# A causal convolution by 128-column blocks: a second level of three products for four, its shared product drained by ScalarE and GpSimd

## The chip, the cores and the metric

The kernel runs on one core of a Trainium2 chip. The metric is device time in microseconds (us), the median of several runs. TensorE (PE in the profile) multiplies, VectorE (DVE) and ScalarE (ACT) do elementwise work, GpSimd (POOL) does small work and issues some DMAs, SyncE (SP) issues the others. One execution was also recorded by the hardware profiler; all durations of single instructions come from that one.

## The reference, cut to what matters

The input x has 2048 rows of 1024. After a layer norm, two branches are added to x: a feed-forward layer with int4 weights, and a causal convolution along each row with one kernel K of 1024 taps, which is computed from small state-space parameters.

```python
K = _s4_kernel(Lambda, p, q, B, Ct, step, L).astype(u.dtype)
n = 2 * L
y = jnp.fft.irfft(jnp.fft.rfft(u, n=n) * jnp.fft.rfft(K, n=n), n=n)[..., :L]
return y + D[0] * u
...
x = x + _L0_attn_ref(xn, ...) + _L0_ffn_ref(xn, ...)
```

Written as a matrix product, output column block j (128 columns) of a row is the sum over k up to j of input block k times a 128x128 block that depends on j - k alone.

## The kernel before, in words

Every large product is made of float16 pairs: a float32 value is kept as a high half and a low half, and a product takes three matmuls (high by high, high by low, low by high; the list PASS). The kernel has three stages. The first computes the norm, the gate and the up projection and the hidden layer, the second the convolution, the third the down projection. The second stage is the one that changes: `conv` and `last_tiles` (lines 1215 and 1240) in the loop of lines 1275 to 1297.

The convolution works on 32 output tiles of 128 rows by 512 columns. They are numbered by cp (which 1024 rows), c (which 512 of these), hh (which half of the columns) and q (which 128 rows). The transposed normalised input `xc` holds, for each 512 rows and each half, four blocks of 128 columns. `band` (line 1185) holds the convolution's taps laid out so that a run of its columns is a row of neighbouring blocks of the matrix.

A tile is built in two steps. `conv` takes a PSUM bank (`cv`) and adds the part of the output that comes from the same half: input block k goes to all the columns from 128k on, so the matmuls are 512, 384, 256 and 128 columns wide, three of each. For the upper half (hh = 1) it also adds what comes from the lower half. That is a product of two by two blocks of 256, done with three products: two with differences of the taps (`diff`, lines 1205 to 1209), twelve matmuls of 256 columns, in the same bank, and one with the sums of the inputs, `xs`, in a bank of its own (`cc`, lines 1254 to 1258, six matmuls of 256 columns). `last_tiles` adds the last 64 and 128 rows of the down projection to the bank `cv` (five matmuls of 512 columns, `hpl` by `wp`), loads the tile of x into `o` (named p in the profile), and VectorE adds the bank to it (line 1252). For the upper half VectorE then adds the bank `cc` to both 256-column halves of `o` (line 1260). SP stores `o`.

Two loops order this. In the first 1024 rows (cp = 0) `last_tiles` of a tile stands four tiles behind its `conv`; in the second it follows at once, and after each group of four tiles `prepare` brings up operands of the third stage. The sums `xs` for all of cp stand before the loop, four calls of `add_split` (line 1193: three additions, a copy on ScalarE, a subtraction).

The order in which each engine's instructions stand is decided before the run by a planner: in this part of the program nothing is pinned, and the planner goes through its own expected times and puts next what it expects to be ready, with the order of the program as the priority.

The buffers that matter: eight PSUM banks under one tag (line 1123); ten buffers `hb` for 512 float32 columns (line 1122), from which the two `diff`, all temporaries `t` and all tiles `o` are taken; six `f` buffers for `x7`, `xs` and the factors `a` and `s` of the third stage (line 1118); five `g` buffers, one of which holds `hpl` in the second 1024 rows (line 1119); three `be` buffers, which hold `band` and the two `wp` (line 1120).

The third stage is a list of 49 products of 60 matmuls of 256 columns each. Product (1, 6), the third of them, needs the sum of two factors (line 1166), which takes a fifth `f` buffer after the four factors.

Of the kernel before, what the change touches and what calls it, by code (L numbers as in the profile page):

```python
# [24 lines left out]
F16 = mybir.dt.float16  # L25
# [3 lines left out]
AF = mybir.ActivationFunctionType  # L29
# [58 lines left out]
def build(nc, tc, x, xp, raw_d, sz_d, par_d, vct_d, tab_d, csrow_d, out):  # L88
# [3 lines left out]
    with es:  # L92
# [15 lines left out]
        def htile(name, tag="h"):  # L108
            return pools["h"].tile([P, 512], F32, tag=tag, name=name)
# [1074 lines left out]

        band = bep.tile([P, 2, 1024], F16, tag="be", name="band")
        for b in range(2):
# [6 lines left out]
        def add_split(dst, srcs, op):  # L1193

            (h0, l0), (h1, l1) = srcs
            n = dst.shape[2]
            t = htile("t")[:, 0:n]
            V.tensor_tensor(t, h0, h1, op)
            V.tensor_tensor(t, t, l0, ALU.add)
            V.tensor_tensor(t, t, l1, op)  # L1200
            A.copy(dst[:, 0], t)
            V.tensor_tensor(dst[:, 1], t, dst[:, 0], ALU.subtract)


        diff = []
        for a0, b0 in ((128, 384), (640, 384)):
            a, b = ([band[:, i, c : c + 384] for i in range(2)] for c in (a0, b0))
            diff.append(htile(f"diff{a0}").bitcast(F16).rearrange("p (a b) -> p a b", a=2)[:, :, 0:384])
            add_split(diff[-1], (a, b), ALU.subtract)
        wp = []  # L1210
        for i in range(2):
            wp.append(bep.tile([P, 2, 1024], F16, tag="be", name=f"wp{i}"))
            SP.dma_start_transpose(wp[i].rearrange("p b (c d) -> p (b c) d", d=P), WPN[:, i])

        def conv(cp, c, hh, q, xc):

            ts = slice(q * P, (q + 1) * P)
            ps = bank(f"cv{cp}{c}{hh}{q}")
            first = [True]

            def mm(dst, w, m):
                PE.matmul(dst, w, m, start=first[0], stop=False, skip_group_check=True)
                first[0] = False

            xt = xc[2 * c + hh]
            for k in range(4):
                for xi, bi in PASS:
                    mm(ps[:, P * k : 512], xt[:, xi, k, ts], band[:, bi, 0 : 512 - P * k])
            if hh:

                xt = xc[2 * c]
                for k in range(2):
                    for xi, bi in PASS:
                        mm(ps[:, 0:256], xt[:, xi, k + 2, ts], diff[0][:, bi, P - P * k : P - P * k + 256])
                for k in range(2):
                    for xi, bi in PASS:
                        mm(ps[:, 256:512], xt[:, xi, k, ts], diff[1][:, bi, P - P * k : P - P * k + 256])
            return ps

        def last_tiles(ps, cp, c, hh, q, hpl, xs):  # L1240

            ts = slice(q * P, (q + 1) * P)
            cols = slice(512 * hh, 512 * hh + 512)
            mm = lambda w, m, stop=False: PE.matmul(ps, w, m, start=False, stop=stop, skip_group_check=True)
            for hi, wi in PASS:
                mm(hpl[:, c, hi, ts], wp[0][:, wi, cols])
            mm(hpl[:, c, 2, ts], wp[1][:, 0, cols])
            mm(hpl[:, c, 2, ts], wp[1][:, 1, cols], True)
            t0 = 1024 * cp + 512 * c + P * q
            o = htile(f"p{cp}{c}{hh}{q}")  # L1250
            SP.dma_start(o, x[t0 : t0 + P, cols])
            V.scalar_tensor_tensor(o, ps, osc, o, ALU.mult, ALU.add)
            if hh:
                pc = bank(f"cc{cp}{c}{q}")
                for k in range(2):
                    for n, (xi, bi) in enumerate(PASS):
                        PE.matmul(pc[:, 0:256], xs[:, c, xi, k, ts], band[:, bi, 512 - P * k : 768 - P * k],
                                  start=(k == 0 and n == 0), stop=(k == 1 and n == 2))
                ov = o.rearrange("p (a b) -> p a b", a=2)
                V.scalar_tensor_tensor(  # L1260
                    ov, pc[:, 0:256].unsqueeze(1).to_broadcast([P, 2, 256]), osc, ov, ALU.mult, ALU.add)
            SP.dma_start(out[t0 : t0 + P, cols], o)
# [12 lines left out]
        for cp in range(2):  # L1275
# [5 lines left out]
            xc = [xf[cp, 3], xf[cp, 1], x7, xf[cp, 0]]  # L1281
            xs = fp.tile([P, 2, 2, 2, 512], F16, tag="f", name=f"xs{cp}")
            for c in range(2):
                for k in range(2):
                    a, b = ([xc[2 * c][:, i, m, :] for i in range(2)] for m in (k, k + 2))
                    add_split(xs[:, c, :, k, :], (a, b), ALU.add)

            behind = []
            for c, hh in ((0, 0), (0, 1), (1, 1), (1, 0)) if cp == 0 else ((0, 1), (0, 0), (1, 1), (1, 0)):
                for q in range(4):  # L1290
                    behind.append((conv(cp, c, hh, q, xc), cp, c, hh, q))
                    if len(behind) > 4 - 4 * cp:
                        last_tiles(*behind.pop(0), hpl, xs)
                if cp:
                    prepare()
            while behind:
                last_tiles(*behind.pop(0), hpl, xs)

# [206 lines left out]
```

## Time and profile before

| what | us |
|---|---|
| median of 3 runs | 1290.91 (1290.76 to 1292.72) |
| the profiled execution, its own time | 1293.54 |
| its span, first to last instruction | 1291.5 |
| PE busy in the span | 1258.9 (97%) |
| DVE busy | 1007.7 (78%) |
| ACT busy | 672.1 (52%) |
| POOL busy | 177.4 (14%) |
| first and last start of a matmul into `cv` | 846.6 and 966.1 |

The span is shorter than the execution's time by 2.0 us, which lie around it. "Busy" counts the time in which at least one instruction of the engine was under way. Matmuls overlap in the record: one of 512 columns is shown with 379 ns, though the next starts 216 ns later, so it is the distance of starts that tells what a matmul costs in a row of matmuls. The convolution stage lies between about 846 and 967 us of the span. There GpSimd does nothing, and ScalarE is busy for a tenth of the time.

### The profile page before, as it was taken

What the parts mean: (1) busy time and instruction counts of PE and PEld (TensorE: products, weight loads), DVE (VectorE), ACT (ScalarE), POOL (GpSimd) and SP (SyncE); (2) the same over time, 40 slices, a digit from 0 to 9 for tenths busy, and PEclk for the clock granted to TensorE, in tenths of its full rate; (3) what the DMA queues carried; (4) which work ended last, traced back from release to release, by engine and by line L of the source; (5) the groups of instructions that cost most, each with busy time, mean ns of one, the idle gap of its engine ahead of it and who ended that gap; (6) DMA issues with size and microseconds to landing.
All of it is one profiled execution on the core that took longest, in us unless ns stands there. A gap on an engine that the chain in (4) does not pass through costs nothing. (4 is left out here: it accounts for less than half of the span.)

```text
span 1291.5 us, 20871 instructions
## 1 busy us (share of the span) xinstructions
PE 1258.9 (97%) x7880; PEld 753.2 (58%) x7880; DVE 1007.7 (78%) x1344; ACT 672.1 (52%) x1208; POOL 177.4 (14%) x267
## 2 busy tenths in 40 slices
PE   5999999999999999999998999999999999999998
PEld 5744344444444444444443444456668888888887
DVE  6789974888978788878788887663758898779792
ACT  4868476666657556656666675620105433443330
POOL 2230010200010000100010001000000131356440
PEclk8999999999999999999999999999999999999999
DMA  6692938789795959889998998775938778999981
GB/s 222 147 227 59 203 101 157 213 218 239 162 252 144 253 146 241 224 209 235 244 239 216 260 243 201 226 264 183 350 122 344 239 230 226 256 283 259 288 176 50
DMA packets 358401, 276.04 MB, mean 214 GB/s; under 512 B 211668, under 2 KB 304668, under 8 KB 354204
## 3 DMA queue, kind: packets, MB, share of 16 engines
q1 hardware_dynamic: 335676, 261.59, 74.1%
q0 software_dynamic: 21760, 10.49, 6.9%
q10 hardware_dynamic: 864, 2.62, 0.5%
q8 instruction: 62, 1.02, 0.3%
q14 instruction: 39, 0.32, 0.1%
HBM read 132.36 MB, written 94.84 MB: 176 GB/s over the span
## 5 line engine op out<-in xcount | busy, mean ns | idle before, releaser
L82 PEld LDWEIGHTS <-wf 128*128 128x128 f16 x2807 | 274.0, 98 | 341.0 <-issue 7.0
L77 PEld LDWEIGHTS <-g 128*128 128x128 f16 x2940 | 287.7, 98 | 33.5
L82 ACT ACTIVATE w<-w,sz 128x64 f32<-128x64 int32 x560 | 196.0, 428 | 68.4 <-DVE w L82 51.3
L77 ACT CAST g<-a 128x2560 f16<-128x2560 f32 x42 | 97.5, 2324 | 176.6 <-PE A L77 50.4
L82 PE MATMUL D<-x,wf 128*128 128x512 f16 x816 | 188.0, 380 | 0.9 <-ACT D L82 0.9
L77 PE MATMUL A<-b,g 128*128 128x256 f16 x1680 | 185.9, 273 | 0.0
L82 PE MATMUL A<-x,wf 128*128 128x512 f16 x791 | 177.7, 380 | 5.1 <-DMA wf<-nat 4.7
L82 PE MATMUL C<-x,wf 128*128 128x512 f16 x804 | 179.1, 379 | 0.0
L82 DVE TENSOR_TENSOR w<-w 128x256 f32<-128x256 f32 (+1 forms) x244 | 132.6, 544 | 39.5 <-ACT w L82 32.3
L77 PEld LDWEIGHTS <-wf 128*128 128x128 f16 x1152 | 100.1, 100 | 98.4 <-DMA wf<-nat 4.3
L77 DVE TENSOR_TENSOR g<-a,g 128x2560 f16<-128x2560 f32 x42 | 118.5, 2823 | 29.6 <-ACT g L77 29.6
L1357 POOL DMA_DIRECT2D out<-o x64 | 78.8, 2127 | 320.7 <-DVE o L77 309.8
L82 ACT CAST nd<-w 128x896 f16<-128x896 f32 x70 | 65.2, 932 | 82.8 <-DVE w L82 65.6
L322 POOL TENSOR_SCALAR sz<-sz 128x16 f32<-128x16 f32 x42 | 16.5, 392 | 632.8 <-DMA sz<-in_sz 586.5
L77 PE MATMUL D<-b,g 128*128 128x256 f16 x840 | 94.0, 273 | 0.0
L82 PE MATMUL B<-x,wf 128*128 128x512 f16 x396 | 90.9, 379 | 2.1 <-ACT B L82 2.1
L82 DVE TENSOR_TENSOR nd<-w,nd 128x896 f16<-128x896 f32 x70 | 76.1, 1086 | 9.2 <-ACT nd L82 9.2
L82 ACT CAST nat<-w 128x896 f16<-128x896 f32 x62 | 55.2, 936 | 34.1 <-ACT B L82 17.0
L77 PEld LDWEIGHTS <-x 128*128 128x128 f16 x576 | 53.4, 98 | 25.0 <-issue 1.1
L82 DVE TENSOR_TENSOR nat<-w,nat 128x896 f16<-128x896 f32 x62 | 64.8, 1085 | 1.5 <-ACT nat L82 1.5
L77 PE MATMUL cv<-band,x 128*128 128x512 f16 (+3 forms) x384 | 57.1, 299 | 1.0 <-DVE hb L82 1.0
L77 DVE SCALAR_TENSOR_TENSOR p<-cv,p 128x512 f32<-128x512 f32 x32 | 22.0, 689 | 43.3 <-PE cv L77 33.6
(169 smaller groups left out, 1408.6 us busy)
## 6 DMA issues: line engine op xcount, KB each, us to landing
a<-HF SPq DMA_DIRECT2D x28, 1280.0 KB, 8.0
WD<-nd SPq DMA_DIRECT2D x70, 448.0 KB, 4.1
b<-WD SPq DMA_DIRECT2D x49, 640.0 KB, 6.0
w<-SZT SPq DMA_DIRECT2D x80, 256.0 KB, 5.4
raw<-in_raw SPq DMA_DIRECT2D x65, 256.0 KB, 4.0
HF<-ha SPq DMA_DIRECT2D x54, 256.0 KB, 3.4
HF<-s SPq DMA_DIRECT2D x40, 256.0 KB, 2.8
HF<-hb SPq DMA_DIRECT2D x36, 256.0 KB, 3.6
```

The lines of the kernel that those rows point to most:

```text
L77: return method(*args, **kw)
L82: self.last = method(*args, **kw)
L322: G.tensor_scalar(sz[:, 0], sz[:, 0], WS, None, ALU.mult)
L1357: G.dma_start(dst, o[:, q], accum_op=ALU.add)
```

## The change

The two by two block products of 256 columns are split once more, into 128-column blocks with three products in place of four.

In `conv`, the own half is now computed directly only inside each 256-column block (matmuls of 256, 128, 256 and 128 columns, three of each). What goes from the first 256 columns to the second is a two by two block product, made of two products with the difference tables `near` (in `last_tiles`, six matmuls of 128 columns by `crossed`) and one shared product with the sum of two input blocks. For the upper half, each of the two products with `diff` is split in the same way: twelve matmuls of 128 columns with `far[0]` and `far[1]` in `conv`, and two shared products. All shared products, six matmuls of 256 and nine of 128 columns for an upper tile and three of 128 for a lower one, go to a second bank (`cc`), now for each tile.

That bank is no longer read by VectorE. ScalarE copies it, scaled, into a new buffer `u` from the `hb` pool, and GpSimd adds `u` to `o` (two additions over 512 columns for an upper tile, one over 256 for a lower one), before VectorE adds the bank `cv`.

The tables `near` and `far` are made by `outer_less_middle` (three subtractions and additions of 256 columns, a copy on ScalarE, a subtraction), in the spare columns of the `be` buffers. The sums of inputs are made by `block_sums`: five per 512 rows of cp and c, in one `f` buffer for each c; the one for c = 0 stands before the loop, the one for c = 1 before the second group of tiles. A sum is one addition of the high halves, a copy on ScalarE, a subtraction, and two additions in float16.

```diff
--- before.py
+++ after.py
@@ -1182,7 +1182,12 @@
             return gsplit(src, f"g{k}_{m}"), b
 
 
-        band = bep.tile([P, 2, 1024], F16, tag="be", name="band")
+        def table(name):
+
+            t = bep.tile([P, 2560], F16, tag="be", name=name)
+            return t[:, 0:2048].rearrange("p (a b) -> p a b", a=2), t[:, 2048:2560].rearrange("p (a b) -> p a b", a=2)
+
+        band, near = table("band")
         for b in range(2):
             for n in range(2):
                 p0 = 64 * b + 32 * n
@@ -1193,72 +1198,112 @@
         def add_split(dst, srcs, op):
 
             (h0, l0), (h1, l1) = srcs
-            n = dst.shape[2]
-            t = htile("t")[:, 0:n]
+            t = htile("t")[:, 0:384]
             V.tensor_tensor(t, h0, h1, op)
             V.tensor_tensor(t, t, l0, ALU.add)
             V.tensor_tensor(t, t, l1, op)
             A.copy(dst[:, 0], t)
             V.tensor_tensor(dst[:, 1], t, dst[:, 0], ALU.subtract)
 
-
+        def outer_less_middle(dst, src):
+
+            t, sub = htile("t")[:, 0:256], ALU.subtract
+            t3 = t.rearrange("p (a b) -> p a b", a=2)
+            part = [src[:, i].rearrange("p (k d) -> p k d", d=P) for i in range(2)]
+            mid = [part[i][:, 1:2].to_broadcast([P, 2, P]) for i in range(2)]
+            V.tensor_tensor(t3, part[0][:, 0:3:2], mid[0], sub)
+            V.tensor_tensor(t3, t3, part[1][:, 0:3:2], ALU.add)
+            V.tensor_tensor(t3, t3, mid[1], sub)
+            A.copy(dst[:, 0], t)
+            V.tensor_tensor(dst[:, 1], t, dst[:, 0], sub)
+
+        wp, far = [], []
         diff = []
         for a0, b0 in ((128, 384), (640, 384)):
             a, b = ([band[:, i, c : c + 384] for i in range(2)] for c in (a0, b0))
             diff.append(htile(f"diff{a0}").bitcast(F16).rearrange("p (a b) -> p a b", a=2)[:, :, 0:384])
             add_split(diff[-1], (a, b), ALU.subtract)
-        wp = []
+        outer_less_middle(near, band[:, :, 128:512])
         for i in range(2):
-            wp.append(bep.tile([P, 2, 1024], F16, tag="be", name=f"wp{i}"))
-            SP.dma_start_transpose(wp[i].rearrange("p b (c d) -> p (b c) d", d=P), WPN[:, i])
+            w, f = table(f"wp{i}")
+            wp.append(w)
+            far.append(f)
+            SP.dma_start_transpose(w.rearrange("p b (c d) -> p (b c) d", d=P), WPN[:, i])
+            outer_less_middle(f, diff[i])
+
+        def block_sums(cp, c, xc):
+
+            sm5 = fp.tile([P, 5, 2, 512], F16, tag="f", name=f"xs{cp}{c}")
+            lower, upper = xc[2 * c], xc[2 * c + 1]
+            add = ALU.add
+            for i, (xt, a, b) in enumerate(((lower, 0, 1), (upper, 0, 1), (lower, 2, 3), (lower, 0, 2), (lower, 1, 3))):
+                dst, t = sm5[:, i], htile("t")
+                t16 = t.bitcast(F16)[:, 0:512]
+                V.tensor_tensor(t, xt[:, 0, a], xt[:, 0, b], add)
+                A.copy(dst[:, 0], t)
+                V.tensor_tensor(dst[:, 1], t, dst[:, 0], ALU.subtract)
+                V.tensor_tensor(t16, xt[:, 1, a], xt[:, 1, b], add)
+                V.tensor_tensor(dst[:, 1], dst[:, 1], t16, add)
+            return sm5
+
+        def crossed(ps, xt, k, col, pair, ts):
+
+            for xi, bi in PASS:
+                for n in range(2):
+                    c0 = col + P * n
+                    PE.matmul(ps[:, c0 : c0 + P], xt[:, xi, k + 1 - n, ts], pair[:, bi, P * n : P * n + P],
+                              start=False, stop=False, skip_group_check=True)
 
         def conv(cp, c, hh, q, xc):
 
             ts = slice(q * P, (q + 1) * P)
             ps = bank(f"cv{cp}{c}{hh}{q}")
-            first = [True]
-
-            def mm(dst, w, m):
-                PE.matmul(dst, w, m, start=first[0], stop=False, skip_group_check=True)
-                first[0] = False
-
             xt = xc[2 * c + hh]
             for k in range(4):
-                for xi, bi in PASS:
-                    mm(ps[:, P * k : 512], xt[:, xi, k, ts], band[:, bi, 0 : 512 - P * k])
+                lo, hi = P * k, 256 * (k // 2) + 256
+                for n, (xi, bi) in enumerate(PASS):
+                    PE.matmul(ps[:, lo:hi], xt[:, xi, k, ts], band[:, bi, 0 : hi - lo],
+                              start=(k == 0 and n == 0), stop=False, skip_group_check=True)
             if hh:
-
-                xt = xc[2 * c]
-                for k in range(2):
-                    for xi, bi in PASS:
-                        mm(ps[:, 0:256], xt[:, xi, k + 2, ts], diff[0][:, bi, P - P * k : P - P * k + 256])
-                for k in range(2):
-                    for xi, bi in PASS:
-                        mm(ps[:, 256:512], xt[:, xi, k, ts], diff[1][:, bi, P - P * k : P - P * k + 256])
+                crossed(ps, xc[2 * c], 2, 0, far[0], ts)
+                crossed(ps, xc[2 * c], 0, 256, far[1], ts)
             return ps
 
-        def last_tiles(ps, cp, c, hh, q, hpl, xs):
+        def last_tiles(ps, cp, c, hh, q, hpl, xc, xs):
 
             ts = slice(q * P, (q + 1) * P)
             cols = slice(512 * hh, 512 * hh + 512)
             mm = lambda w, m, stop=False: PE.matmul(ps, w, m, start=False, stop=stop, skip_group_check=True)
+            pc = bank(f"cc{cp}{c}{hh}{q}")
+            shared = [(256, 0, band[:, :, 256:384])]
+            if hh:
+                shared = [(384, 1, band[:, :, 256:384]), (256, 2, diff[0][:, :, P : 2 * P]), (384, 0, diff[1][:, :, P : 2 * P])]
+                for k in range(2):
+                    for n, (xi, bi) in enumerate(PASS):
+                        PE.matmul(pc[:, 0:256], xs[:, 3 + k, xi, ts], band[:, bi, 512 - P * k : 768 - P * k],
+                                  start=(k == 0 and n == 0), stop=False, skip_group_check=True)
+            for i, (col, src, w) in enumerate(shared):
+                for n, (xi, bi) in enumerate(PASS):
+                    PE.matmul(pc[:, col : col + P], xs[:, src, xi, ts], w[:, bi],
+                              start=(not hh and n == 0), stop=(i == len(shared) - 1 and n == 2), skip_group_check=True)
+            crossed(ps, xc[2 * c + hh], 0, 256, near, ts)
             for hi, wi in PASS:
                 mm(hpl[:, c, hi, ts], wp[0][:, wi, cols])
             mm(hpl[:, c, 2, ts], wp[1][:, 0, cols])
             mm(hpl[:, c, 2, ts], wp[1][:, 1, cols], True)
             t0 = 1024 * cp + 512 * c + P * q
-            o = htile(f"p{cp}{c}{hh}{q}")
+            o, u = htile(f"p{cp}{c}{hh}{q}"), htile(f"u{cp}{c}{hh}{q}")
             SP.dma_start(o, x[t0 : t0 + P, cols])
+            used = slice(0, 512) if hh else slice(256, 384)
+            A.activation(u[:, used], pc[:, used], AF.Copy, scale=osc)
+            ov = o.rearrange("p (a b d) -> p a b d", a=2, b=2)
+            if hh:
+                G.tensor_tensor(o.rearrange("p (a b) -> p a b", a=2), o.rearrange("p (a b) -> p a b", a=2),
+                                u[:, 0:256].unsqueeze(1).to_broadcast([P, 2, 256]), ALU.add)
+                G.tensor_tensor(ov, ov, u[:, 256:512].rearrange("p (a d) -> p a d", a=2).unsqueeze(2).to_broadcast([P, 2, 2, P]), ALU.add)
+            else:
+                G.tensor_tensor(ov[:, 1], ov[:, 1], u[:, 256:384].unsqueeze(1).to_broadcast([P, 2, P]), ALU.add)
             V.scalar_tensor_tensor(o, ps, osc, o, ALU.mult, ALU.add)
-            if hh:
-                pc = bank(f"cc{cp}{c}{q}")
-                for k in range(2):
-                    for n, (xi, bi) in enumerate(PASS):
-                        PE.matmul(pc[:, 0:256], xs[:, c, xi, k, ts], band[:, bi, 512 - P * k : 768 - P * k],
-                                  start=(k == 0 and n == 0), stop=(k == 1 and n == 2))
-                ov = o.rearrange("p (a b) -> p a b", a=2)
-                V.scalar_tensor_tensor(
-                    ov, pc[:, 0:256].unsqueeze(1).to_broadcast([P, 2, 256]), osc, ov, ALU.mult, ALU.add)
             SP.dma_start(out[t0 : t0 + P, cols], o)
 
         items = [(k, m) for k in SEQ for m in (1, 2, 6, 5, 7, 4, 3)]
@@ -1279,22 +1324,22 @@
             x7 = fp.tile([P, 2, 4, 512], F16, tag="f", name=f"x7_{cp}")
             SP.dma_start(x7, XSP[cp])
             xc = [xf[cp, 3], xf[cp, 1], x7, xf[cp, 0]]
-            xs = fp.tile([P, 2, 2, 2, 512], F16, tag="f", name=f"xs{cp}")
-            for c in range(2):
-                for k in range(2):
-                    a, b = ([xc[2 * c][:, i, m, :] for i in range(2)] for m in (k, k + 2))
-                    add_split(xs[:, c, :, k, :], (a, b), ALU.add)
-
+            xs = {0: block_sums(cp, 0, xc)}
             behind = []
-            for c, hh in ((0, 0), (0, 1), (1, 1), (1, 0)) if cp == 0 else ((0, 1), (0, 0), (1, 1), (1, 0)):
+            order = ((0, 0), (0, 1), (1, 1), (1, 0)) if cp == 0 else ((0, 1), (0, 0), (1, 1), (1, 0))
+            for i, (c, hh) in enumerate(order):
+                if i == 1:
+                    xs[1] = block_sums(cp, 1, xc)
                 for q in range(4):
                     behind.append((conv(cp, c, hh, q, xc), cp, c, hh, q))
                     if len(behind) > 4 - 4 * cp:
-                        last_tiles(*behind.pop(0), hpl, xs)
+                        b = behind.pop(0)
+                        last_tiles(*b, hpl, xc, xs[b[2]])
                 if cp:
                     prepare()
             while behind:
-                last_tiles(*behind.pop(0), hpl, xs)
+                b = behind.pop(0)
+                last_tiles(*b, hpl, xc, xs[b[2]])
 
 
         U = [uxp.tile([P, 4, 512], F32, tag="ux", name=f"U{cp}") for cp in range(2)]
```

## The prediction

> **What bounds the kernel now.** I read the page first, for the engines' shares:
>
> ```profile
> PE 1258.9 (97%) x7880; PEld 753.2 (58%) x7880; DVE 1007.7 (78%) x1344; ACT 672.1 (52%) x1208; POOL 177.4 (14%) x267
> ```
>
> TensorE is busy for 97% of the span, but that is an average over stages, so next the table of windows over the convolution (window, length, then busy time and instructions of PE, PEld, DVE, ACT and POOL, then clock, DMA share, GB/s):
>
> ```profile
> 846.00:857.00 11.00, 9.83 (x71) 6.10 (x69) 8.30 (x16) 2.84 (x5) 0.00 (x0) 1.00 0.79 269
> 857.00:860.00 3.00, 2.89 (x19) 1.70 (x20) 3.00 (x7) 0.00 (x0) 0.00 (x0) 1.00 0.94 294
> ...
> sum 121.00, PE 119.72 PEld 78.15 DVE 71.02 ACT 12.73 POOL 0.00; mean PE 9.21 PEld 6.01 DVE 5.46 ACT 0.98 POOL 0.00
> ```
>
> TensorE idles for 1.28 us of 121, all of it before 857.2, at full clock. The stage costs what its matmuls cost. Their prices are distances of starts in the timeline of TensorE (start, length, what, count):
>
> ```profile
> 896.23 1.79 PE L77 MATMUL cv<-band,x 128*128 128x512 f16 x12
> 897.86 1.24 PE L77 MATMUL cv<-wp,hpl 128*128 128x512 f16 x5
> 898.94 0.82 PE L77 MATMUL cc<-band,xs 128*128 128x256 f16 x6
> 899.60 1.79 PE L77 MATMUL cv<-band,x 128*128 128x512 f16 x12
> ```
>
> Five of 512 columns take 897.86 to 898.94: 0.216 us each. Six of 256 take 0.66: 0.109 each. For 128 columns there is a run of 48 early in the kernel:
>
> ```profile
> 50.49 0.83 PE L77 MATMUL g<-x,wf 128*128 128x128 f16 x12
> 51.16 0.83 PE L77 MATMUL u<-x,wf 128*128 128x128 f16 x12
> 51.83 0.83 PE L77 MATMUL g<-x,wf 128*128 128x128 f16 x12
> 52.50 0.83 PE L77 MATMUL u<-x,wf 128*128 128x128 f16 x12
> ```
>
> Twelve take 0.67: 0.056 each. The twelve matmuls of an own half take 1.63, which leaves 0.162 for 384 columns. So a matmul costs its columns and some 0.003 us, although each has a weight load of its own.
>
> **TensorE's sum.** A lower tile before: 3 x (0.216 + 0.162 + 0.109 + 0.056) + 5 x 0.216 = 2.71 us. An upper tile has 18 of 256 columns more: 4.67. Sixteen of each: 118.1. A lower tile after: own half 6 x 0.109 + 6 x 0.056 = 0.99; shared product and `near` 9 x 0.056 = 0.50; `wp` 1.08; together 2.57. An upper one: 0.99; crossed 12 x 0.056 = 0.67; bank `cc` 6 x 0.109 + 9 x 0.056 = 1.16; `near` 0.34; `wp` 1.08; together 4.24. Sixteen of each: 109.0. That is 384 more matmuls, and **-9.2 us** if nothing else comes late.
>
> A page of the Trainium skill speaks against the change here: TensorE: Matmul & The Clock Gate, section Back-to-back issue gap, says that a stream of pairs of weight load and matmul at 128 columns sustains about 81 ns each. By it the 672 added matmuls of 128 columns would cost 16.8 us more, and the change would lose 7.6 us on TensorE alone. The run above has a weight load per matmul and shows 56 ns; the measurement decides.
>
> **VectorE and ScalarE in the middle of the stage: hidden.** VectorE's operations on 512 float32 columns start 0.60 apart when nothing holds them (903.14, 903.74, 904.34 in its timeline). Gone are 16 additions of bank `cc` (9.6 us) and 32 operations for `xs` (19.2). Added are 20 sums: two operations of 0.60 each, and two all in float16, a form that the trace has at 1024 columns (0.69 against 1.22 for float32), so about 0.35: 1.9 in all, 38 us. The three tables add 12 operations of 256 columns at 0.34: 4.1. So +13 us on 71 of 118. ScalarE gets 32 copies `u` (0.43 to 0.60, its rows of 64 and 512 columns) and 15 more casts (0.51 to 0.62): +24 us on 13. TensorE's work covers both, except at the start.
>
> **GpSimd: hidden, if an addition stays well under 2.8 us (rival 3).** It has no row of this size. The nearest:
>
> ```profile
> L323 POOL TENSOR_TENSOR sz<-sz 128x16 f32<-128x16 f32 x42 | 15.7, 376 | 3.2
> L125 POOL TENSOR_SCALAR_AFFINE_SELECT ident<-ident 128x128 f32<-128x128 f32 x1 | 0.3, 282 | 0.1
> ```
>
> From below: VectorE's 0.60 for 512 columns. Taken: four times the 128-column row, 1.13. From above: twice that for the second input, 2.26, and 0.9 us of waiting, since the 128x16 addition takes 0.22 alone and up to 1.12 under VectorE: 3.2. At 1.13 an upper tile needs 2.26 of GpSimd's time against 4.24 of TensorE's, a lower one 0.6 against 2.57. VectorE's last addition queues behind GpSimd's on the way to the store, and SP's queue, which issues stores and loads in order, behind that; eight banks at two a tile leave some three tiles of slack.
>
> **The start: where part of the gain is lost.** From the timeline of all engines:
>
> ```profile
> 847.18 10.70 SPq L77 DMA_DIRECT2D p<-in_x  x4
> 849.40 6.68 PE L77 MATMUL cv<-band,x 128*128 128x512 f16 x48 [1.01 <-DVE hb L82]
> 850.64 0.55 DVE L77 TENSOR_TENSOR t<-band 128x384 f32<-128x384 f16 x1
> 857.11 1.25 PE L77 MATMUL cv<-wp,hpl 128*128 128x512 f16 x5 [0.27 <-DMA hpl<-HPL]
> 861.04 0.69 DVE L77 SCALAR_TENSOR_TENSOR p<-cv,p 128x512 f32<-128x512 f32 x1
> ```
>
> The load of `hpl` ends at 857.1 whatever the convolution does, and until then TensorE lives on own halves: five of 1.63, and seven matmuls with `diff`. After the change an own half is 0.99. In program order tiles 0 to 5 with two banks `cc` fill the eight banks, so six own halves, 5.9 us, last from 846.6 (with the 1.0 of idle that is there) to 853.6. `far` and `near` are not ready: VectorE starts on the tables at 850.64 and needs 3.8 us for `diff` and 4.1 for the rest. So TensorE idles 3.5 us in place of 0.27: **+3.3** (0.3 less if all eight banks take own halves, which ends at 855.5: +1.4 is the lower end).
>
> Then the banks. All ten sums of cp = 0 stand ahead of the first last addition in the program: VectorE has them done at 850.64 + 3.8 + 4.1 + 19 = 877.5. The temporaries also stand ahead of the first `o` and `u` in the ten buffers. That this order binds is shown by the second 1024 rows: all 16 loads of p stand ahead of the next temporary, which waited for a store:
>
> ```profile
> 898.49 0.69 DVE L77 TENSOR_TENSOR t<-x 128x512 f32<-128x512 f16 x1 [2.02 <-DMA out<-p]
> ```
>
> So `o` of tile 0 is loaded when the third sum is done, at about 864, lands at 868 (3.7 us is the loads' median), and its bank comes free between 869 and 878. TensorE has, with the bank that `u` of tile 0 frees at 866, work until about 870.5; a second `cc` gives it three more. It loses between 0 and 4.6 us. Before, the first last addition (861.04) came among the sums and 2.8 us after its matmuls, so neither end is plain; I take the middle, **+2.3**.
>
> **The handover.** Before, the sum `s` for product (1, 6) starts at 955.7, when `xs` is dead. After, `xs` and x7 live to the last tile, so it starts about 1.4 us before the stage ends. Three operations of 2.73, one last addition of 0.6, a cast of 2.3 and a subtraction of 2.8 end 12.5 us after the stage; the product is due after two others, 2 x 6.55 = 13.1. I take **+0.3**; bounds 0 and 2.
>
> **Sum.** -9.2 + 3.3 + 2.3 + 0.3 = -3.3 us. The profiled execution took 1293.54 (span 1291.5 and 2.0 around it), so it would become 1290.2. It lies 2.6 above the median of the runs; the same step from 1290.91 gives **1287.6**.
>
> **Rivals.**
> 1. The start stays covered: own halves fill eight banks (+1.4), last additions slip in among the sums (0), the handover costs nothing: -7.8, 1283.1. For it: the planner puts next what is ready. Against: VectorE's list at the start more than doubles. Chance 0.22.
> 2. The start eats it all: VectorE runs its sums to the end, 3.3 + 4.6, and the handover takes 1.3: 0.0, 1290.9. For it: program order is the priority, and the sums are always ready. Chance 0.17.
> 3. Slower: GpSimd becomes the bound of the upper tiles. At p us for an addition of 512 columns an upper tile needs 2p and a lower one p/2, 40p in all, against TensorE's 109. Single upper tiles outlast TensorE's 4.24 from 2.1 on, which the lower ones and the slack of three tiles make good; the whole is slower than before once 40p exceeds 109 + 3.3, from 2.8. At 2.9 that is 116 - 109 - 3.3 = +3.7, 1294.6; at the upper bound of 3.2, +15.7, 1306.6. For it: the 128x16 addition goes from 0.22 to a mean of 0.38 beside VectorE. Against: it needs 2.5 times my price. Chance 0.20, most of it near the lower end.
> That the change does not do what it says is hardly a case: the columns are counted from the code.
>
> **Numbers.** The forecast's own range is -1 to -5.5, chance 0.41. A measurement of this kernel can tell about 0.2%, 2.6 us, from no change. Faster than that: rival 1 and three quarters of the forecast, 0.52; within it: the rest of the forecast, rival 2 and a little of rival 3, 0.29; slower: 0.19. The range reaches from rival 1 to the milder half of rival 3: 1282.5 to 1296.
>
> **What would show it.** Right: starts of 128-column matmuls 0.056 apart in the stage, the starts of the last tile's matmuls 3 to 4 us earlier than 966.1 in the span, idle of TensorE before 857.1 near 4 to 5 us and some more before 880, GpSimd additions near 1.1 us, VectorE not waiting for GpSimd with a full queue behind. Wrong: 128-column matmuls at more than 0.07; idle of TensorE spread over the stage, with GpSimd above 9 tenths (rival 3); no idle after 857 (rival 1); a hole ahead of product (1, 6) of over 2 us.

## The result, and the profile after

The changed kernel takes **1309.7 us** (median of 4 runs, 1306.71 to 1309.91) where the kernel before took 1291.26 beside it (4 runs): ratio **1.0136, 95% interval 1.0118 to 1.0153**. The forecast was 1287.6 with a range up to 1296. The profiled execution took 1309.75 with a span of 1307.8: 16.3 more than the span before.

Lines of the page of the changed kernel: the engines' shares, and the granted clock by fortieths of the span.

```profile
PE 1259.5 (96%) x8264; PEld 767.2 (59%) x8264; DVE 1024.4 (78%) x1388; ACT 694.2 (53%) x1255; POOL 239.9 (18%) x315
...
PEclk8999999999999999999999999979999999999999
```

TensorE is busy as long as before, with 9 us less to do. The dip of the clock row lies in the convolution. The table of windows over that stage, columns as in the prediction:

```profile
846.00:857.00 11.00, 4.62 (x52) 4.10 (x52) 8.73 (x18) 3.40 (x6) 0.00 (x0) 0.88 0.97 339
857.00:860.00 3.00, 2.96 (x22) 2.40 (x21) 3.00 (x7) 2.19 (x5) 0.00 (x0) 0.50 0.04 10
860.00:870.00 10.00, 8.24 (x50) 4.66 (x50) 10.00 (x24) 2.69 (x6) 0.00 (x0) 0.60 0.08 26
...
940.00:950.00 10.00, 5.62 (x47) 4.11 (x46) 9.31 (x13) 4.74 (x5) 6.15 (x4) 0.82 1.00 344
```

Before, TensorE was busy for 9.83 of the first eleven microseconds at full clock; now for 4.62, and from 854.3 to 868.0 it runs at half clock. A second gap lies at 940 to 950.

**The account used below.** From each matmul of the stage to the next I take the distance of starts less the price of its columns (0.216, 0.162, 0.109, 0.056 us for 512, 384, 256 and 128). What is left is lost time, and I add it up over four parts: start (the first 30 us of the stage), middle (30 to 58), late (58 to the end), third (the first 25 us of the third stage). It holds idle time and slow clock together. Before: 1.6, 0, 0, 0. Changed: **13.6, 5.1, 8.3, 2.2**. So 27.6 us more are lost, TensorE's own sum is 9.2 less, and the stage began 1.9 earlier (844.7; it begins between 841 and 850 in the profiles here, from what lies ahead of it): 16.5, against 16.3 in the span.

The start in TensorE's timeline:

```profile
847.43 4.12 PE L77 MATMUL cv<-band,x 128*128 128x256 f16 x48 [1.62 <-DVE hb L82]
856.50 0.39 PE L77 MATMUL cc<-band,xs 128*128 128x128 f16 x2 [4.95 <-ACT xs L77]
...
860.63 0.58 PE L77 MATMUL cv<-wp,x 128*128 128x128 f16 x4 [0.68 <-ACT wp L77]
862.34 0.58 PE L77 MATMUL cv<-band,x 128*128 128x128 f16 x4 [1.12 <-DVE band L77]
862.72 2.34 PE L77 MATMUL cv<-wp,hpl 128*128 128x512 f16 x5
864.85 0.63 PE L77 MATMUL cv<-band,x 128*128 128x128 f16 x4
```

Five own halves are done at 851.6. Then TensorE waits 4.95 us for the first sum, and for shorter times for the tables (`far` is in `wp`, `near` in `band`). The four holes are 8.4 us (1.3 in the kernel before). Behind 862.34 TensorE waits for nothing until 883.0. The other 5.2 are slow matmuls: the five of 512 columns at 862.72 take 2.13 to the next start, 0.426 each, twice their price. The granted clock was half from 854.3 to 868.0.

GpSimd's rows over the stage (busy, mean ns of one, then idle before and its releasers), and what VectorE's last additions waited for (total, times, longest):

```profile
L1303 POOL TENSOR_TENSOR p<-p,u 128x512 f32<-128x512 f32 x16 | 21.5, 1350 | 0.6
L1301 POOL TENSOR_TENSOR p<-p,u 128x512 f32<-128x512 f32 x16 | 20.6, 1296 | 27.3 <-ACT u L77 22.1 <-DMA p<-in_x 5.2
L1305 POOL TENSOR_TENSOR p<-p,u 128x256 f32<-128x256 f32 x16 | 20.1, 1254 | 88.2 <-DMA p<-in_x 75.7 <-ACT u L77 6.1 <-issue 3.7
```

```profile
DVE p L77 <- POOL p L1303: 37.3, 12, 7.1
...
DVE p L77 <- POOL p L1305: 11.6, 9, 2.7
...
PE cv L77 <- DVE p L77: 6.4, 2, 4.4
```

GpSimd works 62 us of 136, so it is not the bound, but VectorE's last additions wait 49 us for it, and TensorE twice for them. The longer of those two, in the timeline of all engines:

```profile
942.21 4.23 DVE L77 TENSOR_TENSOR t<-x 128x512 f32<-128x512 f16 x3
...
942.77 3.38 POOL L1303 TENSOR_TENSOR p<-p,u 128x512 f32<-128x512 f32 x2
...
946.96 0.68 DVE L77 SCALAR_TENSOR_TENSOR p<-cv,p 128x512 f32<-128x512 f32 x1
...
947.69 2.72 PE L77 MATMUL cv<-band,x 128*128 128x256 f16 x18 [4.38 <-DVE p L77]
```

The operations of VectorE's sums (`t`) and GpSimd's additions run at once and slow each other. The row of three `t` holds two of float32, which took 1.16 and 1.75 us in place of 0.69, and one of float16, 1.48 in place of 0.41; GpSimd's additions took 1.7 each in place of 1.26 (one at 936.97 with no sum beside it). The last addition that frees the bank comes behind the sums, at 946.96. Undisturbed, the three `t` start 0.60, 0.60 and 0.34 apart, 1.5 us in place of the 4.15 to the next start, so some 2.6 of the 4.38 us are their own delay (an estimate).

### The profile page after: what moved, and what is told of

The parts are those of the page before. It is cut to its first block, busy times and chain, and to the rows that moved or that the text cites. A ratio compares the mean times of both kernels' runs of the same rounds, so it can differ in the third digit from the quotient of the medians.

```text
span 1307.8 us, 21862 instructions
## 1 busy us (share of the span) xinstructions
PE 1259.5 (96%) x8264; PEld 767.2 (59%) x8264; DVE 1024.4 (78%) x1388; ACT 694.2 (53%) x1255; POOL 239.9 (18%) x315
## 5 line engine op out<-in xcount | busy, mean ns | idle before, releaser
L77 PEld LDWEIGHTS <-x 128*128 128x128 f16 x768 | 58.0, 102 | 20.1 <-issue 12.2
L77 PE MATMUL cv<-band,x 128*128 128x128 f16 (+1 forms) x576 | 56.2, 247 | 9.3 <-DVE p L77 6.4
```

The source lines that it names most:

```text
L77: return method(*args, **kw)
```

## The experiments

All medians stand beside runs of the kernel before on the same chip (medians 1291.3 to 1293.4), so ratios are compared. The account is of the one profiled execution of each kernel, which can lie off the median: e13's took 1295.50 (its stage began at 850.1, the latest of all), e10's 1302.94, e2's 1305.91, e7's 1294.03. `*` marks kernels with the old start.

| kernel | median us | ratio (95%) | start, middle, late, third |
|---|---|---|---|
| changed | 1309.70 | 1.0136 (1.0118-1.0153) | 13.6, 5.1, 8.3, 2.2 |
| e1_vector_drain | 1299.83 | 1.0040 (1.0025-1.0055) | 13.4, 0, 6.3, 0.3 |
| e2_13_buffers | 1308.41 | 1.0107 (1.0087-1.0127) | 15.3, 1.3, 6.5, 3.2 |
| e3_late_sums | 1304.30 | 1.0080 (1.0060-1.0100) | 11.4, 1.4, 9.2, 0.8 |
| e4_first_tiles_old * | 1298.24 | 1.0033 (1.0020-1.0046) | 1.7, 4.3, 7.6, 0.8 |
| e5_old_start_vector * | 1293.63 | 0.9993 (0.9983-1.0002) | 1.7, 6.1, 1.3, 0.3 |
| e6_old_start_vector_13 * | 1288.61 | 0.9960 (0.9944-0.9977) | 1.2, 1.7, 1.1, 0.3 |
| e7_no_gpsimd_add | 1296.42 | 1.0021 (1.0011-1.0031) | 12.3, 0, -0.1, 0.1 |
| e8_old_start_13 * | 1292.54 | 0.9993 (0.9981-1.0005) | 1.2, 0, 4.0, 4.8 |
| e9_before_13 | 1292.36 | 0.9997 (0.9986-1.0007) | 1.5, 0, 0, 0 |
| e10_gpsimd_aside | 1298.56 | 1.0042 (1.0025-1.0059) | 13.5, 4.0, 2.3, 0.1 |
| e11_first_four_old | 1299.04 | 1.0041 (1.0028-1.0054) | 9.8, 4.1, 2.4, 0.3 |
| e12_bank_first | 1308.10 | 1.0119 (1.0104-1.0134) | 12.5, 4.6, 8.8, 0.5 |
| e13_bank_first_old_start_13 * | 1289.49 | 0.9972 (0.9962-0.9982) | 1.1, 0, 5.4, 0.8 |
| e14_bank_first_13 | 1301.75 | 1.0068 (1.0051-1.0086) | 16.7, 0, 6.0, 1.1 |
| e15_bank_first_old_start * | 1297.21 | 1.0036 (1.0023-1.0050) | 1.6, 3.0, 7.6, 1.0 |
| e16_own_u * | 1296.16 | 1.0033 (1.0023-1.0044) | 2.0, 1.9, 8.6, 0.8 |
| e17_four_by_vector * | 1290.51 | 0.9989 (0.9977-1.0000) | 1.2, 0, 5.8, 0.9 |

**The start: e3, e4, e11.**

e3_late_sums makes the sums of the second 512 rows one group of tiles later:

```diff
-                if i == 1:
+                if i == 2:
                     xs[1] = block_sums(cp, 1, xc)
```

e4_first_tiles_old computes the first eight tiles (cp = 0, c = 0) as the kernel before did: with wide matmuls and `diff`, without `near`, `far` and the first three sums; a lower tile needs no bank `cc`:

```diff
+            if cp == 0 and c == 0:
+                for k in range(4):
+                    for n, (xi, bi) in enumerate(PASS):
+                        PE.matmul(ps[:, P * k : 512], xt[:, xi, k, ts], band[:, bi, 0 : 512 - P * k],
...
+                            PE.matmul(ps[:, 256 * part : 256 * part + 256], xc[2 * c][:, xi, k + 2 - 2 * part, ts],
...
```

e11_first_four_old is e6 (below) with only the first four, lower, tiles the old way, and all five sums at the start.

> Only the second set of five sums is moved one group of tiles later in the program, behind the first four last additions. If the sums' place ahead of the last additions holds up the first loads and banks: the 5 us between 875 and 902 go, in the second 1024 rows the sums may come too late by as much: 1303 to 1307. If the start is lost to the tables and the first five sums alone: 1308 to 1311.

> The first eight tiles (first 512 rows) are computed as before the change: own halves directly, two products with the differences over 256 columns, no near or far, two sums in place of five; the rest as after the change. This gives TensorE its old cover at the start and costs 2.3 us of the matmuls' gain. Theory A (the start costs 12 us, half clock included): no hole over 1.5 us before 875, no half clock there, 1298 to 1302. Rival (the loss is made in the middle by GpSimd and buffers): 1308 to 1312.

> As the fastest so far (VectorE drains, thirteen buffers), but only the first four tiles, all lower ones, are computed as before the change, in place of eight; all five sums stand at the start again. 1.7 us less of TensorE's work. If the start needs cover for the own halves alone: 1285 to 1288. If tables and five sums must have come before the upper tiles' part of it: 1290 to 1296, with a hole before 870.

e4 takes the loss of the start from 13.6 to 1.7 us. TensorE's timeline there is that of before again, with full clock throughout:

```profile
854.39 0.93 PE L77 MATMUL cv<-diff,x 128*128 128x256 f16 x7
855.65 0.82 PE L77 MATMUL cv<-wp,hpl 128*128 128x512 f16 x3 [0.34 <-DMA hpl<-HPL]
```

e3, which only takes five sums out of the way, brings 2.2 back at the start. It also takes the middle loss from 5.1 to 1.4, with ten buffers and with GpSimd's additions as they were: the place of the sums in VectorE's list is part of that loss too. In e11 the own halves last, but the upper tiles' table (`far`) is still late, and the time, 1299.04, is above both of the ranges that were expected:

```profile
868.36 2.62 PE L77 MATMUL cv<-wp,x 128*128 128x128 f16 x24 [4.42 <-DVE wp L77]
```

So the start needs long matmuls for as long as VectorE makes tables and sums, not only until `hpl` lands.

**Who adds the shared products: e1, e7, e10.**

e1_vector_drain has no `u` and nothing on GpSimd; VectorE reads the bank in three additions (one for a lower tile):

```diff
+                V.scalar_tensor_tensor(o2, pc[:, 0:256].unsqueeze(1).to_broadcast([P, 2, 256]), osc, o2, ALU.mult, ALU.add)
+                for i in range(2):
+                    w = pc[:, 256 + P * i : 384 + P * i].unsqueeze(1).to_broadcast([P, 2, P])
+                    V.scalar_tensor_tensor(ov[:, i], w, osc, ov[:, i], ALU.mult, ALU.add)
...
```

e7_no_gpsimd_add leaves GpSimd's three additions away, and e10_gpsimd_aside makes additions of the same size inside `u`:

```diff
-                G.tensor_tensor(o.rearrange("p (a b) -> p a b", a=2), o.rearrange("p (a b) -> p a b", a=2),
...
+                G.tensor_tensor(u, u, u, ALU.add)
+                G.tensor_tensor(u, u, u, ALU.add)
...
```

> The bank of shared products is read by VectorE again, as before the change; no copy u, no GpSimd addition, so no temporary buffer for u either. Theory A (the start: VectorE's longer list of tables and sums empties TensorE, whose clock then halves; about 12 of the 27 us lost): the losses after 875 us of the span, about 13 us, may go, the start stays: 1296 to 1299. Theory B (the way through ScalarE, GpSimd and its buffers is not what delays the middle; VectorE's sums are): 1307 to 1313, since VectorE gets 25 us of work more. By the prediction's own words GpSimd is hidden: 1309.

> The kernel after the change with GpSimd's additions left out: the shared products are computed and copied by ScalarE, but not added, so the output lacks them. Buffers, sums, tables and order of the program are the changed kernel's. If GpSimd's time and its contention with VectorE make the 13 us lost after the start: sums' first additions back at 0.69 us from 0.81, losses after 875 us of the span under 5, 1298 to 1302. If the places of u in the ten buffers and the late sums make them: 1305 to 1310.

> The kernel after the change, in which GpSimd makes additions of the same sizes inside u and does not touch the tile of x, so the output lacks the shared products. VectorE's last addition no longer waits for GpSimd, but GpSimd is as busy beside it. If contention (each slows the other) makes the 13 us after the start: 1305 to 1310, sums' first additions at 0.8 us. If the wait in VectorE's queue for GpSimd's result and the later release of banks and buffers make it: 1296 to 1300, near the run without GpSimd additions.

e7 shows that in the changed kernel everything behind the start hangs on GpSimd's additions: 15.6 us of loss go to 0, while the copies `u` stay. It takes away three things at once: the two engines slowing each other, VectorE's waits for GpSimd, and the time for which `o` and `u` are held. The stage is then 121.2, which less 12.2 of loss is 109.0, the prediction's sum for TensorE. e10 leaves 6.4 in its profiled execution; by the medians it is 2.1 us above e7. Its additions run (1.09 us in the mean for 512 columns, so GpSimd is somewhat less busy than in the changed kernel), no last addition waits for them, and they still slow VectorE's sums (785 ns in the mean; 691 in e7, 814 in the changed kernel). That is not all of it: its first hole in the middle ends with a copy `u` that had waited for an operation of VectorE's sums.

```profile
882.01 0.28 ACT L77 ACTIVATE u<-cc 128x128 f32<-128x128 f32 x1 [5.96 <-DVE xs L77]
882.34 1.15 PE L77 MATMUL cv<-band,x 128*128 128x256 f16 x12 [2.20 <-ACT u L77]
```

In e1 VectorE's three reads of the bank do no harm in the middle; most of what is left comes at one place:

```profile
904.72 0.69 DVE L77 TENSOR_TENSOR t<-x 128x512 f32<-128x512 f16 x1 [5.46 <-DMA out<-p]
905.33 1.47 DVE L77 SCALAR_TENSOR_TENSOR p<-cc,p 128x512 f32<-128x512 f32 x3
```

A sum waits for a buffer that a store still reads, and the additions that free banks stand behind it.

**The ten buffers: e2, e5, e6, e8, e9.**

```diff
-        pools["h"] = poolb("hb", bufs=10)
+        pools["h"] = poolb("hb", bufs=13)
```

This alone is e2 (on the changed kernel), e8 (on e4) and e9 (on the kernel before). e5 is e4 with e1's additions; e6 is e5 with 13 buffers.

> Only the ten buffers hb become thirteen. Theory A' (loads of x come late because temporaries and copies u stand ahead of them in ten buffers): the first loads are issued before 860 instead of at 867.9, and the hole at 889 and most of the 5 us lost between 875 and 902 go: 1303 to 1306. Rival (VectorE's time, not its buffers): within 1.5 us of 1309.7.

> Both parts of the last two runs: the first eight tiles as before the change, and VectorE reads the bank of shared products. If the losses at the start and on the way through GpSimd are separate, they add: the 4.3 us that the run with old first tiles still lost between 30 and 58 us after the stage's start go, the hole where a sum on VectorE waits for a store (3.5 us in the second 1024 rows) stays: 1291 to 1295. Rival (VectorE has too much to do once it drains all banks): 1296 to 1300.

> The same with thirteen buffers hb in place of ten. If the remaining hole is a sum that waits for a buffer, ahead of last additions in VectorE's queue, it goes: 1286 to 1290. If it is VectorE's time: as with ten, 1291 to 1295.

> First eight tiles as before the change, drain through ScalarE and GpSimd, thirteen buffers hb. With the three others a square of drain by buffers. If late loads of x make the loss in the middle: 1291 to 1294. If GpSimd's slowness beside VectorE makes it: 1296 to 1299.

> The kernel before the change with thirteen buffers hb: a control for the fastest kernel so far, which has thirteen as well. TensorE idles only 1.3 us in that stage before, so buffers alone should give nothing: within 1.5 us of the kernel before. If they give 4 us, that kernel's gain is not the matmuls'.

Three more buffers are worth nothing before (e9) but take away most of the middle loss in each pair: 5.1 to 1.3, 6.1 to 1.7, 4.3 to 0. The 6.1 of e5 is mostly the hole that e1 has, where a sum waits 5.5 us for a store: it lies 50 us into the stage in e5 and 59 in e1, just behind the bound at 58. e2 itself came out where its rival had it, 1308.4: its first loads of x were issued at 868.8 and not before 860, and start and third lost more than in the changed kernel. **e6 is faster than both kernels** (so is e13, below). Its table of windows at the start:

```profile
846.00:857.00 11.00, 10.02 (x75) 6.48 (x73) 9.47 (x19) 3.91 (x7) 0.00 (x0) 1.00 0.85 283
857.00:860.00 3.00, 3.00 (x26) 2.25 (x25) 3.00 (x7) 2.89 (x6) 0.00 (x0) 1.00 0.78 311
860.00:870.00 10.00, 10.00 (x86) 7.11 (x83) 10.00 (x25) 0.81 (x2) 0.00 (x0) 1.00 0.47 151
```

No gap but the one of about 1 us that the kernel before has too, and no half clock; VectorE is as busy as in the changed kernel.

**The order of the last two additions: e12 to e15.**

```diff
             A.activation(u[:, used], pc[:, used], AF.Copy, scale=osc)
+            V.scalar_tensor_tensor(o, ps, osc, o, ALU.mult, ALU.add)
             ov = o.rearrange("p (a b d) -> p a b d", a=2, b=2)
...
-            V.scalar_tensor_tensor(o, ps, osc, o, ALU.mult, ALU.add)
```

e12 is this on the changed kernel, e14 with 13 buffers; e15 and e13 the same two on e4.

> The changed kernel with the last two steps of a tile exchanged: VectorE adds the bank `cv` to `o` first, which frees the bank without a wait for GpSimd; then GpSimd adds `u` to `o`, then the store. The same work on every engine, and VectorE and GpSimd can still slow each other. If the loss behind the start (13.4 us in the changed kernel) is mainly VectorE's queue standing behind GpSimd's result, it falls to 6 or less (e10_gpsimd_aside, which has that contention and no such wait, lost 6.3), and the time is 1298 to 1302. If it is mainly the contention, or the buffers that come back late because the store still waits for GpSimd, 10 or more stays and the time is 1305 to 1310. The start is the same in both: some 13 us.

> e8_old_start_13 (first eight tiles computed the old way, 13 buffers, bank `cc` through ScalarE and GpSimd) with VectorE's last addition ahead of GpSimd's. e8_old_start_13 lost 4.0 us late in the stage and 4.8 in the third stage. If both come from VectorE's queue behind GpSimd, 1 to 3 us in all are left and the time is about 1286 to 1288, the same as or better than with VectorE reading the bank itself (1288.6). If they come from contention or from late buffers, nothing moves: 1291 to 1294.

> e12_bank_first with 13 `hb` buffers in place of ten. In e12_bank_first the loss behind the start stayed (13.4 us), so VectorE's queue is not its only cause: in its trace a bank waits for a last addition (881.9), that waits for a load of x which SP issued at 880.6, behind two stores whose tiles GpSimd had just finished, with all ten buffers taken. If the queue behind GpSimd and the late buffers are two causes each of which is enough alone, taking away both leaves 3 to 7 us (as in e10_gpsimd_aside, 6.3) and the time is 1297 to 1301, though the buffers alone (e2_13_buffers) and the order alone (e12_bank_first) gave 1 to 3 us. If it is the contention between GpSimd and VectorE, it stays at 1305 or more. The start is disturbed as before.

> e13_bank_first_old_start_13 with ten buffers: the missing corner of the square of order and buffers on the kernels with the old start (GpSimd first and 10 buffers 1298.2, GpSimd first and 13 buffers 1292.5, bank first and 13 buffers 1289.5). By late buffers with ten of them whatever the order, 1296 to 1299. If the order is worth the same 3 us at ten buffers, 1295.

After e7 and e10 my theory was that VectorE's queue, standing behind GpSimd, makes the loss. **e12 refutes it as the only cause**: the last additions wait 6 us for GpSimd in place of 49, but 18 for loads of x in place of 0.5, and 13.4 us are lost in the middle and late as before. Its timeline shows the next thing in line:

```profile
876.33 3.82 POOL L1306 TENSOR_TENSOR p<-p,u 128x256 f32<-128x256 f32 x1 [0.39 <-DVE t L77]
...
880.63 1.13 SPq L77 DMA_DIRECT2D p<-in_x  x2
...
884.22 0.69 DVE L77 SCALAR_TENSOR_TENSOR p<-cv,p 128x512 f32<-128x512 f32 x1 [4.65 <-DMA p<-in_x]
884.96 1.76 PE L77 MATMUL cc<-band,xs 128*128 128x256 f16 x9 [3.09 <-DVE p L77]
```

The tile's store waits for GpSimd (3.82 us for an addition that takes 0.72 alone), the next load of x for the store's buffer, and the bank for the load. With ten buffers the order moves nothing that is clear of the noise (ratios 1.0136 and 1.0119; old start 1.0033 and 1.0036), with 13 it gives 0.4% and 0.2% (1.0107 to 1.0068, 0.9993 to 0.9972). The buffers give 0.3 to 0.6%. In the account the loss behind the start is 15.6 in the changed kernel, 14.0 with the order alone (e12), 11.0 with the buffers alone (e2) and 7.1 with both (e14): 8.5 together, 6.2 as a sum of the two. That each hides a part of the other is likely, but by the ratios this part is 0.2%, about the size of their intervals. With both, middle is 0 and third about 1, but the late loss stays, 5.4 and 6.0.

**The late loss: e16, e17.**

Both start from e13. e16_own_u goes back to ten `hb` buffers and takes `u` from three of its own:

```diff
+            u = None if pc is None else pools["h"].tile([P, 512], F32, tag="u", bufs=3, name=f"u{cp}{c}{hh}{q}")
```

e17_four_by_vector has e1's additions for four tiles:

```diff
+            vec = cp == 1 and c == 0 and hh == 1
...
+            if vec:
...
```

> e13_bank_first_old_start_13 with the 13 buffers parted: three for `u` alone, ten for the rest. In every kernel in which GpSimd does the additions, 4 to 9 us are lost late in the stage, at about 90 us of it, where the sums of the last 512 rows stand on VectorE; in e13_bank_first_old_start_13 5.4, with a hole of 3.1 that waits for a copy `u`. If the copy is late because `u` takes its buffer in turn behind the sums' temporaries, the late loss falls to 2 or less and the time is about 1286. If the two engines slow each other there (contention), 4 or more stay and the time is 1289 to 1291.

> e13_bank_first_old_start_13 with the four upper tiles that stand ahead of those sums (cp = 1, c = 0, hh = 1) read by VectorE from the bank `cc`, so that GpSimd has nothing to do while the sums run; VectorE has about 5 us more. If contention makes the late loss (5.4), it falls to 2 or less, VectorE's float32 sums late in the stage take 0.69 us again in place of up to 1.7, and the time is about 1286. If it is the turn of the buffers or too much work on VectorE at that place, 4 or more stay: 1289 to 1291.

Neither settles it. In e16 the late loss is 8.6: the sums, with ten buffers again, wait up to 6.5 us for stores. In e17 VectorE's float32 sums take 719 ns in place of 838 (e13), and yet 5.8 us go, because VectorE now has its own long list there; its timeline, and TensorE's first row behind the hole:

```profile
923.03 2.82 DVE L77 TENSOR_TENSOR g<-a,g 128x2560 f16<-128x2560 f32 x1
...
930.25 0.34 PE L77 MATMUL cc<-band,xs 128*128 128x128 f16 x3 [3.77 <-DVE p L77]
```

An operation of 2.82 us for the third stage, sums and additions from the bank are all due at once. e6, with still more on VectorE, loses 1.1, in another order of its list. So contention (each engine slows the other) goes with this loss in some kernels and the order of VectorE's list in others, and no run parts the two; how the changed kernel's 8.3 divide between them **stays open**.

## Why the prediction failed, step by step

- **TensorE's sum, -9.2: right.** Twelve matmuls of 128 columns in the stage take 0.67 us:

```profile
922.78 0.83 PE L77 MATMUL cv<-wp,x 128*128 128x128 f16 x12
923.45 0.38 PE L77 MATMUL cc<-band,xs 128*128 128x256 f16 x2
```

  e7 confirms the whole sum (109.0), and e6: 109.0, plus 2.3 for eight tiles the old way, plus 4.0 lost, is 115.3; its stage took 115.2.
- **"The start", +3.3 and +2.3: right in place, wrong in size, and in part in cause.** It cost 12.0. The wait for the tables came, at 7.1 us more of holes than before in place of 3.3. I had six own halves until `hpl` lands; there were five. The longest hole, 4.95, ended with the first sum, which my term did not hold at all, and the tables, not `hpl`, ended the two behind it: `near` was written at 861.86 to 862.3, and the `wp` matmuls of the same banks stood behind it. The wait for banks, +2.3, did not come: TensorE waits for nothing from 862.34 to 883.0. I left the clock out wholly, and 5.2 us are slow matmuls. From 862.72 to 868.0 TensorE did not wait, so half clock cost some half of that, 2.6 us (an estimate), and of the rest of the 5.2 a part would have been spent waiting for tables anyway. With 12.0 in place of 5.6 the forecast would have been 1294.0, still inside its range.
- **"GpSimd: hidden": the step that failed.** It put GpSimd's additions at 0 us; they cost 15.6, the third stage's 2.2 among them. The price was nearly right for 512 columns (1.13 taken, 1.30 to 1.35 measured) and too low for 256 (0.6 taken, 1.25 measured, 0.72 with no sum beside it). Rival 3's condition, 2.8 us, was not met; it named the right engine and the wrong mechanism. The sentence that failed is "eight banks at two a tile leave some three tiles of slack". VectorE's queue stood behind GpSimd's additions (49 us of waits), and in the middle the slack was set by the ten buffers, which now hold `o` and `u` of tiles in flight and all temporaries. With GpSimd in the path `o` and `u` are held until it is done; loads, last additions and banks then come late in turn (e12's timeline). Middle and late cost 13.4 us, all of it gone without the additions (e7), most of the middle part gone with three more buffers or with five sums out of the way (e3). The late part is shown to come with the additions; how it comes about stays open.
- **"VectorE and ScalarE in the middle: hidden"** holds for the work by itself: in e6 VectorE has 52 additions more than in e4, all those from `cc`, and 3.1 us are lost behind the start (e4: 12.7). It fails where sums, temporaries and last additions meet in one queue.
- **The handover, +0.3: 2.2**, just over the bound of 2. The sum `s` started 0.2 us behind the stage's end, where I had it 1.4 before, because the last addition ahead of it came at 980.10, behind GpSimd's on the same tile, which had waited 2.77 us for a DMA. VectorE's addition for the last tile then waited for GpSimd until 984.1 (0.61 us), and three operations of 2.8 us stood behind it:

```profile
979.34 0.73 POOL L1305 TENSOR_TENSOR p<-p,u 128x256 f32<-128x256 f32 x1 [2.77 <-DMA out<-p]
...
980.10 0.69 DVE L77 SCALAR_TENSOR_TENSOR p<-cv,p 128x512 f32<-128x512 f32 x1 [2.81 <-DMA out<-p]
...
980.71 2.81 DVE L77 TENSOR_TENSOR s<-a,a 128x2560 f32<-128x2560 f32 x1
...
984.14 0.69 DVE L77 SCALAR_TENSOR_TENSOR p<-cv,p 128x512 f32<-128x512 f32 x1 [0.61 <-POOL p L1305]
984.74 2.82 DVE L77 TENSOR_TENSOR a<-a,a 128x2560 f32<-128x2560 f32 x1
...
996.67 2.58 PE L77 MATMUL A<-b,g 128*128 128x256 f16 x22 [1.00 <-DVE g L77]
```

  With the bank first it is 0.5 to 1.1 (e12 to e15), but 0.8 in e3 and e4 without that, and 0.1 to 0.3 where no last addition waits for GpSimd (e1, e5, e6, e7, e10, e11).
- **Sum.** Predicted -9.2 + 5.6 + 0.3 = -3.3; measured -9.2 + 12.0 + 13.4 + 2.2 = +18.4 in the stage and behind it.

The planner lays out VectorE's list anew for every variant, so each difference holds some change of order too.

## What to carry to other kernels

Saved matmul time arrives only if the engines that prepare the stage and free its buffers also keep up: keep the old, longer form for the first tiles while tables and sums are being made (e4: from 1.0136 of the time before to 1.0033). A drain that is handed to an idle engine lengthens the life of the buffers in its path, so count the buffers in flight, not only the engine's share. Two limits in a row (here queue order and buffers) can hide a part of each other when they are removed one at a time, so try them in a square.

## What the runs showed of the hardware

- **The clock gate.** After the hole that began at 851.6 the granted clock fell to half at 854.3 and stayed there for 13.65 us. All half-clock stretches between 820 and 1010 us in the runs are multiples of 3.41 us (3.4, 6.8, 10.2, 13.65, 17.1). In the four units of this one TensorE was busy for 1.23, 2.73, 2.30 and 3.41 us, so the clock rose behind the first unit without a hole. In the 3.41 us ahead of each of the 26 falls TensorE was busy for 1.4 us at most. Holes of 2.0 to 2.2 us were followed by a fall in the changed kernel, e10 and e11; in e16 a hole of 3.7 was not. The Trainium skill, TensorE: Matmul & The Clock Gate, section What's actually happening, has a window of about 3.4 us that runs freely; after an idle one the clock falls, after a busy one it rises. The unit of 3.41 agrees, but here a window need not be wholly idle for a fall, and a hole shorter than a window brought half clock.
- **GpSimd and VectorE slow each other.** An addition of 128x256 takes 0.72 us alone and up to 4.39 beside VectorE's operations with two inputs (951.85, changed kernel, beside one of 2.81 us for the third stage and then sums). In e14 three operations of VectorE's sums took 5.11 us together, 1.75 each in place of 0.69, and GpSimd's addition beside them 1.72 in place of 1.26:

```profile
937.84 5.11 DVE L77 TENSOR_TENSOR xs<-t,xs 128x512 f16<-128x512 f32 x3
...
939.01 1.72 POOL L1302 TENSOR_TENSOR p<-p,u 128x512 f32<-128x512 f32 x1
```

  The Trainium skill, GPSIMD Engine Reference, section Key points, says that GpSimd shares its way to the on-chip memory (SBUF) with VectorE, and contends with VectorE's instructions that have two inputs there. The runs agree: VectorE's sums have two, and the last addition, with one input in a PSUM bank, kept 0.68 to 0.70 in the mean in every kernel.
